# A convolution stack on one NeuronCore: other queues and another order for its DMA loads

## The chip, the cores and the metric

The kernel runs on one core of one Trainium2 chip. The metric is the time of one execution on the device in microseconds (us), taken as the median of several runs. A profile of one further execution tells where that time goes. PE is TensorE, DVE is VectorE, ACT is ScalarE, POOL is GpSimd and SP is SyncE. DMAs are issued by SP, ACT or POOL, each of which keeps its own queue of instructions in program order.

## The reference

Four layers follow one another on an image batch x of shape (4, 32, 32, 16) in float32. Each layer adds something to x that it computes from a group-normalised copy of x. Layers 0 to 2 are the same computation with other weights:

```python
first = jnp.einsum('ijpq,bpqc->bijc', M2, inputs)
K = jnp.transpose(G, (2, 3, 4, 0, 1, 5)).reshape(kh, kw, c, h * w * f)
shifted = lax.conv_general_dilated(inputs, K, window_strides=(1, 1), padding='SAME', ...)
shifted = shifted.reshape(b, h, w, h, w, f)
diff = jax.nn.relu(inputs[:, :, :, None, None, :] - shifted)
second = jnp.einsum('ijpq,bpqijc->bijc', W2, diff)
return first - L * second
```

M and Wp are 1024 x 1024 matrices and G holds 1024 different 3 x 3 x 16 x 16 filters, so every layer convolves the whole image with 16384 output channels. Layer 3 is a convolution with a 32 x 32 part of an impulse response, which comes from a quotient of two small 2-D polynomials by Fourier transforms, plus a constant tap h0:

```python
H_truncated = jnp.fft.rfft2(b, s=(l1, l2)) / jnp.fft.rfft2(a, s=(l1, l2))
...
Y = jnp.einsum('...hwi,ijhw->...hwj', X, H_full)
```

## The kernel before, in words

**A layer 0 to 2.** The 16384 channels are cut into 128 blocks of 128. For one block and one of the four images ("a pair" below) ten matmuls (line 336) accumulate in PSUM: the filters ga, gb and gn against the image tiles ims, which hold shifted copies of the image, so that the nine taps and 16 channels lie along the partitions. One DVE instruction (line 344) then takes the minimum with zero, multiplies by W and sums along the row. PSUM holds four such results, so PE can run four pairs ahead of DVE.

**Jobs.** conv_layer (line 301) goes through the blocks in jobs of eight, which is one chunk of G (GC = 8). The first two jobs take chunk 0 for images 0 and 1, then for images 2 and 3; the last two do the same with the last chunk; the fourteen jobs between take all four images, 32 pairs each. Inside a job the Python loop over k (0 to 7, one block each) also emits the loads, and since the schedule is written out by hand (manual_schedule), the order of emission is the order on every engine's queue:

- load_w (line 278) loads W for two blocks, 1 MB broadcast over eight groups of partitions, into one of six buffers. In the middle jobs it comes at even k, in the first two jobs at k = 4 and 6.
- load_g (line 239) loads a chunk of G: two halves each of ga and gb, 256 KB each, and g9, 512 KB broadcast. There are two buffers of ga and gb and one of g9. It comes at k = 1 of every job but the first, for the next job's chunk.
- prepare_g (line 257) comes at k = 6: POOL subtracts the middle tap from ga (line 266), ACT casts g9 into gn (line 270) and DVE forms its low part (line 273). PE needs all of them at the next job's start.
- first_term (line 180) is the layer's first einsum, beside the pairs: it loads M, multiplies on PE (line 199), stores the result ft to DRAM as fd in 16 DMAs (line 223), loads it back in another order as xf (line 226) and POOL adds x (line 231). It is a generator; a step of it is emitted after each block of the middle jobs.
- A second generator follows it: impulse_response in layer 0, toeplitz in layer 2.

**The images.** make_image (line 135) normalises two of the four images, writes them to DRAM (line 150 on SP, the edges in lines 154 and 155 on ACT) and loads the shifted copies back with 24 DMAs (line 166), half on SP and half on ACT. At the start of the program G chunk 0 and the first W are issued on SP ahead of all this; three more W follow the first image tiles (lines 506 to 517).

**The last layer's filter.** impulse_response (line 365) transforms on PE, divides on POOL and DVE, stores td to DRAM (line 441, ACT), loads it back transposed as v in 12 DMAs (lines 460 to 462, ACT), multiplies once more (line 470) and stores hd (lines 483 and 489, ACT), rows of 40 elements: 2048 runs of 160 bytes in each of four DMAs. After the v loads it yields three times, so that three blocks of pairs stand between them and line 470 in PE's order. load_toeplitz (line 495) loads hd into a tile t by eight DMAs of 256 runs of 640 bytes, alternately on SP and ACT. Three tiles are loaded by the toeplitz generator during layer 2, the other five in the tail, where 256 matmuls (line 564) finish the output.

**Semaphores of the DMAs.** SP's and ACT's DMAs share eight semaphores in rotation. A DMA waits until the one that used its semaphore before has landed. DMAs of POOL have eight semaphores of their own.

Of the kernel before, what the change touches and what calls it, by code (L numbers as in the profile page):

```python
# [37 lines left out]
P = 128  # L38
# [5 lines left out]
GC = 8  # L44
# [9 lines left out]
def conv_stack_kernel(ctx, tc, x, M, W, G, den, num, h0, cst, dft, one, idp, idq, out):  # L54
# [125 lines left out]
    def first_term(layer, xt):  # L180

        mts = [load_m(layer, 0)]
        yield
        py = small_psum()
        for b in range(B):
            nc.tensor.transpose(py[:, bass.ts(b, P)], yc[b // 2][:, b % 2, :], ident)
        yt = work.tile([P, 8, B, C], F32, tag="yt", name="yt")
        nc.vector.tensor_copy(yt, py.rearrange("k (b p c) -> k p b c", b=B, p=8))
        for pm in range(1, 4):
            mts.append(load_m(layer, pm))  # L190
            yield
        for _ in range(GC - 4):
            yield
        ft = work.tile([P, 2, 8, S], F32, tag="ft", name="ft")
        for part in range(2):
            pf = small_psum()
            for k in range(4):
                for h in range(2):
                    nc.tensor.matmul(  # L199
                        pf[64 * h : 64 * h + 64],  # L200
                        lhsT=yt[:, 4 * part + k].rearrange("k b c -> k (b c)"),
                        rhs=mts[k][:, h, :],
                        start=(k == 0),
                        stop=(k == 3),
                    )
            pv = pf.rearrange("k (cc p q) -> k cc p q", cc=2, p=8)
            if part == 0:
                nc.scalar.copy(ft, pv)
                mts = []
                for pm in range(4, 8):  # L210
                    yield
                    mts.append(load_m(layer, pm))
                for _ in range(GC - 4):
                    yield
            else:
                nc.vector.tensor_tensor(ft, ft, pv, ALU.add)

        fv = fd.rearrange("(p c) b h cc q -> h cc b c p q", p=8)
        for h in range(2):
            for b in range(B):  # L220
                for cc in range(2):
                    at = 64 * h + C * b
                    nc.scalar.dma_start(out=fv[h, cc, b], in_=ft[at : at + C, cc])  # L223
            yield
        xf = work.tile([P, B, NBLK], F32, tag="xf", name="xf")
        nc.scalar.dma_start(
            out=xf.rearrange("p b n -> p (b n)"), in_=fd.rearrange("p b h cc q -> p (b h cc q)")
        )
        yield
        xr = work.tile([P, B, NBLK], F32, tag="xr", name="xr")  # L230
        nc.gpsimd.tensor_tensor(xr, xt, xf, ALU.add)  # L231
        return xr
# [3 lines left out]
    def chunk(layer, ch):  # L236
        return layer + ch // (NBLK // GC), ch % (NBLK // GC)

    def load_g(layer, ch):
        layer, ch = at = chunk(layer, ch)  # L240
        if layer == 3 or at in gr:
            return
        ga = gs.tile([P, GC, P], F32, tag="ga", name="ga")
        gb = gs.tile([P, GC, P], F32, tag="gb", name="gb")
        g9 = gp.tile([P, GC, P], F32, tag="g9", name="g9")
        src = G[layer][:, bass.ts(ch, GC * P)]
        for half in range(2):
            rows = slice(64 * half, 64 * half + 64)
            nc.sync.dma_start(out=ga[rows].rearrange("r n m -> r (n m)"), in_=src[:64])
            nc.sync.dma_start(out=gb[rows].rearrange("r n m -> r (n m)"), in_=src[64:P])  # L250
        nc.sync.dma_start(
            out=g9.rearrange("r n m -> r (n m)"),
            in_=src[P : P + C].unsqueeze(0).to_broadcast([8, C, GC * P]),
        )
        gr[at] = ga, gb, g9
# [19 lines left out]

    wts = []

    def load_w():

        layer, at = divmod(len(wts), NBLK // 2)  # L280
        if layer == 3:
            return
        cc, q = divmod(2 * at, S)
        wt = wp.tile([P, 2, S * S], F32, tag="w", name="w")
        src = W[layer][cc, :, q : q + 2, :].rearrange("p k m -> p (k m)")
        nc.sync.dma_start(
            out=wt.rearrange("p k m -> p (k m)"),
            in_=src.unsqueeze(1).to_broadcast([8, C, 2 * S * S]),
        )
        wts.append(wt)  # L290

    todo = []

# [7 lines left out]
    def conv_layer(layer, xt, finish, side=()):  # L301
# [14 lines left out]
        for job, (blks, batches) in enumerate(jobs):  # L316
            pairs = job < 2, job >= len(jobs) - 2
            for k, blk in enumerate(blks):
                if any(pairs):

                    if k in ((4, 6) if job != len(jobs) - 2 else (0, 2)):
                        load_w()
                elif k % 2 == 0:
                    load_w()
                if job:
                    if k == 1:
                        load_g(layer, blk // GC + 1)
                    if k == 6:
                        prepare_g(layer, blk // GC + 1)
                wt = wts[64 * layer + blk // 2][:, blk % 2, :]  # L330
                for b in batches:
                    pt = pair_psum()
                    for n, (w, im) in enumerate(zip(gt[layer, blk // GC], ims[b // 2])):
                        for half in range(2):
                            rows = slice(64 * half, 64 * half + 64)
                            nc.tensor.matmul(  # L336
                                pt[:, half, :],
                                lhsT=w[rows, blk % GC, :],
                                rhs=im[rows, :, b % 2, :, :S],
                                start=n == 0,  # L340
                                stop=n == 2,
                            )
                    junk = junkp.tile([P, S * S], F32, tag="junk", name="junk")
                    nc.vector.scalar_tensor_tensor(  # L344
                        junk,
                        pt.rearrange("p h m -> p (h m)"),
                        0.0,
                        wt,
                        ALU.min,
                        ALU.mult,  # L350
                        accum_out=acc[b // 2][:, b % 2, blk : blk + 1],
                    )
                    step()
                if not any(pairs):
                    next(beside, None)
            if pairs[1]:
                a = batches[0] // 2
                two = slice(2 * a, 2 * a + 2)
                nc.vector.tensor_tensor(xn[:, two], result["xr"][:, two], acc[a], ALU.add)
                drain()  # L360
                todo.append(finish(a, xn))
                step()
        return xn

    def impulse_response():
# [81 lines left out]
        with tc.tile_pool(name="fs2", bufs=1) as fs:  # L447
# [9 lines left out]
            rows = td.rearrange("k r p (u m) -> u (k r) p m", u=4)  # L457
            for u in range(4):
                g = 32 * u
                nc.scalar.dma_start(out=v[g : g + 1], in_=rows[u, 0:1])  # L460
                nc.scalar.dma_start(out=v[g + 1 : g + 2], in_=rows[u, 32:33])
                nc.scalar.dma_start(out=v[g + 2 : g + 32], in_=rows[u, 2:32])
            yield
            yield
            yield
            for part in range(4):
                pq = pair_psum()
                for h in range(2):
# [11 lines left out]
                )  # L480
                yield
            nc.gpsimd.tensor_tensor(hs[:, :, :, 0], hs[:, :, :, 0], h0s, ALU.add)
            nc.scalar.dma_start(
                out=hd[:, :8].rearrange("(n m) r -> n m r", m=4), in_=hs[:, 0, :4, S:]
            )
            for h in range(2):
                for l in range(2):
                    n = 64 * (2 * h + l)
                    nc.scalar.dma_start(
                        out=hd[n : n + 64, 8:].rearrange("m (q r) -> q m r", r=PITCH),  # L490
                        in_=hs[32 * l : 32 * l + 32, h],
                    )
            yield

    def load_toeplitz(k):

        t = tp.tile([P, C, TQ * PITCH], F32, tag="t", name="t")
        hv = hd.rearrange("(j i) t -> i j t", j=C)
        for p in range(8):
            at = 8 + k * TQ * PITCH - p  # L500
            (nc.sync, nc.scalar)[p % 2].dma_start(
                out=t[p * C : (p + 1) * C], in_=hv[:, :, at : at + TQ * PITCH]
            )
        return t

    load_g(0, 0)
    load_w()
    images = [make_image(a, xs) for a in range(2)]
    for _ in range(4):
        next(images[0])  # L510
    prepare_g(0, 0)
    todo.append(images[0])
    drain()
    for _ in range(3):
        load_w()
    todo.append(images[1])
    step()
    xs = conv_layer(0, xs, make_image, impulse_response())
# [17 lines left out]

    def toeplitz():
        for k in range(3):
            ts.append(load_toeplitz(k))
            yield  # L540

    xs = conv_layer(2, xs, norm3, toeplitz())
# [113 lines left out]
```

## Time and profile before

| what | value |
|---|---|
| median of 3 runs | 3216.66 us (3215.99 to 3217.17) |
| the profiled execution: its time | 3216.64 us |
| the profiled execution: its span | 3214.8 us |
| PE busy | 3148.2 us (98%), 15852 matmuls |
| DVE busy | 2054.8 us (64%) |
| ACT busy | 75.7 us (2%) |
| POOL busy | 171.9 us (5%) |
| mean granted clock of TensorE | 0.994 |
| moved by DMA | 322.18 MB, 100 GB/s in the mean |
| SP's queue | 302.69 MB, 39.2% of 16 engines' span |
| ACT's queue | 17.04 MB, 3.4% |

The profile is one execution. Its busy times are unions of the instructions' spans on an engine; an engine that waits for a semaphore or issues a DMA is not counted as busy, and a q behind the engine's name (SPq, ACTq) marks such sequencer time. The chain goes back from the last instruction to whatever released it, step by step. In the groups and waits, "A <- B" says that A stood until B was done. "PEclk" and the clock column are the share of full speed that the throttle granted TensorE.

### The profile page before, as it was taken

The page shows a single profiled execution, that of the slowest core. Times are in us where ns is not written, and L with a number is a line of the kernel's source. Part 1 is how long each engine was busy: PE and PEld are TensorE (multiplying, and loading weights), DVE is VectorE, ACT ScalarE, POOL GpSimd, SP SyncE. Part 2 cuts the span into 40 slices and gives each one's busy share as a digit, 9 for nine tenths or more (in the row PEclk, how much of TensorE's full clock was granted, in tenths as well). Part 3 has the DMA queues.
Part 4 walks back from the last instruction along what each step waited for, and adds up shares of the span by engine and source line. Part 5 has one row for each costly group of instructions (what it writes and reads, how often), then busy time and mean ns, then how long its engine had stood idle before and what let it go on. Part 6 is the DMA issues. An engine that isn't in the chain of part 4 may idle for free.

```text
span 3214.8 us, 38408 instructions
## 1 busy us (share of the span) xinstructions
PE 3148.2 (98%) x15852; PEld 1678.7 (52%) x15852; DVE 2054.8 (64%) x3294; ACT 75.7 (2%) x98; POOL 171.9 (5%) x124
## 2 busy tenths in 40 slices
PE   6999999999999999999999999999989999999998
PEld 3545566666666544444544445454444444444445
DVE  4666765666666766666666666766656666666660
ACT  0000000000000000000000000000000000000000
POOL 0002310000000000000000000000000000000000
PEclk9999999999999999999999999999999999999999
DMA  6544344343333554333433343365473343333306
GB/s 148 156 115 116 88 109 94 86 103 88 88 98 90 107 154 118 99 89 88 99 96 86 86 105 87 80 143 144 99 127 89 98 99 89 87 99 92 86 1 85
DMA packets 106383, 322.18 MB, mean 100 GB/s; under 512 B 29214, under 2 KB 59360, under 8 KB 81632
## 3 DMA queue, kind: packets, MB, share of 16 engines
q1 hardware_dynamic: 68608, 302.69, 39.2%
q10 hardware_dynamic: 37600, 17.04, 3.4%
q8 instruction: 124, 2.03, 0.3%
q14 instruction: 51, 0.42, 0.1%
HBM read 313.01 MB, written 6.68 MB: 99 GB/s over the span
## 4 chain that ended last, share of the span: by engine, by line
PE 94%; DMA 4%; DVE 1%; ACTq 0%; issue 0%; SPq 0%; POOL 0%; ACT 0%; DVEq 0%; POOLq 0%
PE pt L336 90%; PE pt L564 2%; DMA t<-hd 1%; DMA img<-y 1%; DMA im<-img 1%; PE pt L199 1%; DMA td<-s 1%; DMA v<-td 0%; DMA fd<-ft 0%; DVE junk L344 0%; DMA h0s<-in_h_dram 0%; PE pt L470 0%; ACTq L223 0%; PE pt L387 0%; POOL hs L452 0%
## 5 line engine op out<-in xcount | busy, mean ns | idle before, releaser
L344 DVE SCALAR_TENSOR_TENSOR junk<-pt,w 128x1024 f32<-128x1024 f32 x1536 | 1880.8, 1224 | 1031.7 <-PE pt L336 1017.4
L336 PE MATMUL pt<-im,ga 64*128 64x512 f32 x6144 | 1834.4, 592 | 38.0 <-DMA im<-img 20.5
L336 PE MATMUL pt<-im,gb 64*128 64x512 f32 x6144 | 1824.4, 589 | 0.9 <-DMA im<-img 0.9
L336 PE MATMUL pt<-im,gn 64*128 64x512 f32 x3072 | 1487.7, 807 | 1.9 <-DMA im<-img 1.9
L336 PEld LDWEIGHTS pt<-im,gb 64*128 64x128 f32 x6144 | 706.5, 186 | 737.7 <-issue 705.0
L336 PEld LDWEIGHTS pt<-im,ga 64*128 64x128 f32 x6144 | 708.6, 188 | 422.8 <-DVE junk L344 246.6
L336 PEld LDWEIGHTS pt<-im,gn 64*128 64x128 f32 x3072 | 355.3, 186 | 295.4 <-issue 290.2
L266 POOL TENSOR_TENSOR ga<-ga,cs 128x1024 f32<-128x1024 f32 x48 | 113.4, 2362 | 2215.5 <-DMA ga<-in_G_dram 2153.5
L273 DVE TENSOR_TENSOR gn<-g,gn 32x1024 fp32r<-32x1024 f32 x96 | 118.0, 1229 | 34.3 <-ACT gn L270 32.3
L344 DVE DVE_READ_ACCUMULATOR junk<-pt,w 128x1 f32 x1536 | 127.3, 83 | 0.0
L270 ACT CAST gn<-g 128x1024 fp32r<-128x1024 f32 x48 | 50.2, 1047 | 2318.7 <-DMA g<-in_G_dram 2020.4
L564 PE MATMUL pt<-t,y 128*128 128x512 f32 (+3 forms) x256 | 70.4, 438 | 0.0
L564 PEld LDWEIGHTS pt<-t,y 128*128 128x128 f32 x256 | 44.2, 193 | 26.2 <-issue 16.2
L571 DVE TENSOR_TENSOR xo<-xo,pt 128x512 f32<-128x512 f32 x1 | 0.7, 689 | 70.8 <-PE pt L564 70.8
L199 PE MATMUL pt<-mt,yt 128*64 128x512 f32 x96 | 21.9, 598 | 0.0
L231 POOL TENSOR_TENSOR xr<-x,xf 128x512 f32<-128x512 f32 x3 | 3.8, 1271 | 294.5 <-DMA xf<-fd 294.5
L470 PE MATMUL pt<-v,inv 64*128 64x512 f32 x16 | 8.6, 656 | 7.5 <-DMA v<-td 7.5
L199 PEld LDWEIGHTS pt<-mt,yt 128*64 128x64 f32 x96 | 6.4, 136 | 13.7 <-issue 9.4
L147 POOL COPY e<-y 32x612 f32<-32x612 f32 x6 | 4.2, 693 | 171.7 <-DVE y L146 171.7
L104 PE MATMUL pt<-s,cs 128*128 128x2 f32 x16 | 3.3, 276 | 9.7 <-DVE s L101 9.7
L408 POOL TENSOR_TENSOR H<-H,d 128x256 f32<-128x256 f32 (+1 forms) x10 | 8.2, 825 | 66.6 <-DVE d L413 66.3
L408 POOL TENSOR_TENSOR t<-s 128x256 f32<-128x256 f32 (+1 forms) x15 | 11.3, 754 | 0.0
(57 smaller groups left out, 141.0 us busy)
## 6 DMA issues: line engine op xcount, KB each, us to landing
w<-in_W_dram SPq DMA_DIRECT2D x192, 1024.0 KB
ga<-in_G_dram SPq DMA_DIRECT2D x96, 256.0 KB
gb<-in_G_dram SPq DMA_DIRECT2D x96, 256.0 KB
g<-in_G_dram SPq DMA_DIRECT2D x48, 512.0 KB
mt<-in_M_dram SPq DMA_DIRECT2D x24, 512.0 KB
t<-hd SPq DMA_DIRECT2D x32, 160.0 KB
t<-hd ACTq DMA_DIRECT2D x32, 160.0 KB
im<-img ACTq DMA_DIRECT2D x72, 67.5 KB
```

The lines of the kernel that those rows point to most:

```text
L104: nc.tensor.matmul(pm[:, :2], lhsT=avg, rhs=s, start=True, stop=True)
L147: nc.gpsimd.tensor_copy(ye[a][96:, :, :, 1:, :], ys[a][96:, :, :, :3, :])
L199: nc.tensor.matmul(pf[64 * h : 64 * h + 64], lhsT=yt[:, 4 * part + k].rearrange("k b c -> k (b c)"), rhs=mts[k][:, h, :], start=(k == 0), ...
L231: nc.gpsimd.tensor_tensor(xr, xt, xf, ALU.add)
L266: nc.gpsimd.tensor_tensor(gv, gv, mid.unsqueeze(1).to_broadcast([P, GC * 8, C]), ALU.subtract)
L270: nc.scalar.copy(gn, g9)
L273: nc.vector.tensor_tensor(lo, g9[r : r + 32], lo.bitcast(F32), ALU.subtract)
L336: nc.tensor.matmul(pt[:, half, :], lhsT=w[rows, blk % GC, :], rhs=im[rows, :, b % 2, :, :S], start=n == 0, stop=n == 2,)
L344: nc.vector.scalar_tensor_tensor(junk, pt.rearrange("p h m -> p (h m)"), 0.0, wt, ALU.min, ALU.mult, accum_out=acc[b // 2][:, b % 2, blk : ...
L408: mul = lambda o, u, w: nc.gpsimd.tensor_tensor(o, u, w, ALU.mult)
L470: nc.tensor.matmul(pq[:, h, :], lhsT=inv[two], rhs=v[two, bass.ts(part, 8)].rearrange("g p m -> g (p m)"), start=True, stop=True,)
L564: nc.tensor.matmul(pov[:, :, 8 * cc :], lhsT=y3[:, cc, 31 - dq : 31 - dq + S, :].rearrange("p q b -> p (q b)"), rhs=t[:, :, q * PITCH : q ...
```

## The change

It has four parts, and the arithmetic stays as it is.

1. At the start, the gb halves of G chunk 0 are issued by ACT instead of SP. The first W is no longer issued ahead of the image's store: it is cut into two halves, the first behind that store and ahead of the im loads, the second behind them.
2. In a layer's first job, load_g for chunk 1 is called at k = 3, ahead of the W of k = 4 and 6; until now it came in the second job at k = 1, behind them.
3. The stores fd, the loads xf and v and the stores hd go from ACT's queue to POOL's. Between the v loads and line 470 there are six yields instead of three.
4. The first three Toeplitz tiles, which were issued by SP and ACT in turn, are issued by POOL alone. Those of the tail stay as they were.

POOL's queue thus gets, in each of layers 0 to 2, 16 fd stores and the xf load ahead of line 231's add; in layer 0 also 12 v loads and 5 hd stores; in layer 2 also 24 Toeplitz loads, between that add and the next chunk's line 266. The diff:

```diff
@@ first_term
-                    nc.scalar.dma_start(out=fv[h, cc, b], in_=ft[at : at + C, cc])
+                    nc.gpsimd.dma_start(out=fv[h, cc, b], in_=ft[at : at + C, cc])
             yield
         xf = work.tile([P, B, NBLK], F32, tag="xf", name="xf")
-        nc.scalar.dma_start(
+        nc.gpsimd.dma_start(
             out=xf.rearrange("p b n -> p (b n)"), in_=fd.rearrange("p b h cc q -> p (b h cc q)")
         )
@@ load_g
-    def load_g(layer, ch):
+    def load_g(layer, ch, other=None):
...
-            nc.sync.dma_start(out=gb[rows].rearrange("r n m -> r (n m)"), in_=src[64:P])
+            (other or nc.sync).dma_start(out=gb[rows].rearrange("r n m -> r (n m)"), in_=src[64:P])
@@ load_w
-    def load_w():
+    def load_w(parts=1):
...
-        nc.sync.dma_start(
-            out=wt.rearrange("p k m -> p (k m)"),
-            in_=src.unsqueeze(1).to_broadcast([8, C, 2 * S * S]),
-        )
         wts.append(wt)
+        n = 2 * S * S // parts
+        for k in range(parts):
+            nc.sync.dma_start(
+                out=wt.rearrange("p k m -> p (k m)")[:, bass.ts(k, n)],
+                in_=src[:, bass.ts(k, n)].unsqueeze(1).to_broadcast([8, C, n]),
+            )
+            yield
@@ conv_layer
-                        load_w()
+                        list(load_w())
                 elif k % 2 == 0:
-                    load_w()
-                if job:
-                    if k == 1:
-                        load_g(layer, blk // GC + 1)
-                    if k == 6:
-                        prepare_g(layer, blk // GC + 1)
+                    list(load_w())
+                if k == (3 if job == 0 else 1):
+                    load_g(layer, blk // GC + 1)
+                if job and k == 6:
+                    prepare_g(layer, blk // GC + 1)
@@ impulse_response
-                nc.scalar.dma_start(out=v[g : g + 1], in_=rows[u, 0:1])
-                nc.scalar.dma_start(out=v[g + 1 : g + 2], in_=rows[u, 32:33])
-                nc.scalar.dma_start(out=v[g + 2 : g + 32], in_=rows[u, 2:32])
-            yield
-            yield
-            yield
+                nc.gpsimd.dma_start(out=v[g : g + 1], in_=rows[u, 0:1])
+                nc.gpsimd.dma_start(out=v[g + 1 : g + 2], in_=rows[u, 32:33])
+                nc.gpsimd.dma_start(out=v[g + 2 : g + 32], in_=rows[u, 2:32])
+            for _ in range(6):
+                yield
...
-            nc.scalar.dma_start(
+            nc.gpsimd.dma_start(
                 out=hd[:, :8].rearrange("(n m) r -> n m r", m=4), in_=hs[:, 0, :4, S:]
             )
...
-                    nc.scalar.dma_start(
+                    nc.gpsimd.dma_start(
                         out=hd[n : n + 64, 8:].rearrange("m (q r) -> q m r", r=PITCH),
@@ load_toeplitz
-    def load_toeplitz(k):
+    def load_toeplitz(k, queues=(nc.sync, nc.scalar)):
...
-            (nc.sync, nc.scalar)[p % 2].dma_start(
+            queues[p % len(queues)].dma_start(
                 out=t[p * C : (p + 1) * C], in_=hv[:, :, at : at + TQ * PITCH]
             )
@@ the start of the program
-    load_g(0, 0)
-    load_w()
+    load_g(0, 0, nc.scalar)
+    w0 = load_w(2)
     images = [make_image(a, xs) for a in range(2)]
     for _ in range(4):
         next(images[0])
+    next(w0)
     prepare_g(0, 0)
     todo.append(images[0])
     drain()
+    next(w0)
     for _ in range(3):
-        load_w()
+        list(load_w())
@@ toeplitz
-            ts.append(load_toeplitz(k))
+            ts.append(load_toeplitz(k, (nc.gpsimd,)))
```

## Prediction

> **What bounds the kernel now.** I read the page's chain first, then busy time by stretch, then chain, waits and timeline around each stretch in which PE is not full.
>
> ```profile
> PE 94%; DMA 4%; DVE 1%; ACTq 0%; issue 0%; SPq 0%; POOL 0%; ACT 0%; DVEq 0%; POOLq 0%
> ```
>
> The end is set by PE. A (block, image) pair is ten matmuls; the chain gives 3720 in 732.38 us, so 1.97 us a pair and 62.8 us a job of 32 pairs. The change touches none of these 15360 matmuls (3024 us). It can only touch what PE loses:
>
> ```profile
> 0.00:34.90 34.90, 5.76 (x12) 2.52 (x13) 6.83 (x17) 3.64 (x5) 6.16 (x10) 1.00 0.68 154
> 71.30:125.00 53.70, 49.31 (x235) 35.00 (x236) 30.96 (x49) 1.04 (x1) 2.35 (x1) 0.94 0.68 153
> 440.00:520.00 80.00, 72.52 (x352) 48.04 (x350) 42.00 (x68) 5.68 (x7) 7.34 (x4) 0.94 0.43 96
> 2296.00:2368.00 72.00, 58.95 (x300) 28.12 (x296) 35.21 (x56) 1.04 (x1) 3.60 (x2) 0.93 0.83 113
> ```
>
> The columns are stretch, length, then PE, PEld, DVE, ACT, POOL busy, granted clock, DMA share, GB/s. These four hold nearly all of PE's idle time; in 520 to 1052 and 1166 to 2068 PE is busy throughout. The chain names what is late in the first three:
>
> ```profile
> 10.96 12.46 DMA img<-y
> 46.44 14.34 DMA img<-y
> 101.56 4.39 issue
> 474.46 13.55 DMA v<-td
> ```
>
> The image's store needs 12.46 us because G and the first W stand ahead of it. The landings in the trace (a DMA's last semaphore update) show it: g9 at 13.32, W at 22.57, the store at 23.41. The gap at 101.56 is G chunk 1: issued at 71.0 behind two W, landed at 101.03. At 480.7 PE stands 7.48 us in line 470 until v lands. The fourth, by waits:
>
> ```profile
> ACT gn L270 <- DMA t<-hd: 120.6, 1, 120.6
> DVE gn L273 <- ACT gn L270: 15.9, 1, 15.9
> PE pt L336 <- DVE junk L344: 13.0, 1, 13.0
> ```
>
> ```profile
> 2341.79 21.18 ACTq L501 DMA_DIRECT2D t<-hd  x12
> 2363.06 1.04 ACT L270 CAST gn<-g 128x1024 fp32r<-128x1024 f32 x1 [120.56 <-DMA t<-hd]
> ```
>
> ACT can't cast gn until it has issued its Toeplitz loads, which wait for free semaphores; DVE stands in line 273, and PE runs out of PSUM. Each long pause also costs clock: the records show half speed from 105.0 to 111.8, 483.9 to 494.1 and 2357.8 to 2371.4.
>
> **What the Trainium skill says.** (1) "DMA: Bandwidth & Descriptors", section "Issuing engines are not separate DMA queues": all queues share the same 16 engines, another queue saves only issue time. The trace agrees: the v load that ACT issued at 474.46 landed at 488.02, with SP's W (486.89). (2) "Perfetto Trace Analysis", section "DMA Instruction — SWDGE (GPSIMD)": a GpSimd DMA occupies its cores until the last descriptor is written, so the next POOL instruction waits. No run here shows one. (3) "TensorE: Matmul & The Clock Gate", section "What's actually happening": half clock after an idle window of about 3.4 us. The trace agrees: half clock begins 3.4 us after the gap at 101.56.
>
> **The head.** In the new order x, ga, ga, g9 stand in SP's queue and gb, gb in ACT's: the same 1.5 MB on the same engines, so g9 still lands near 13.3. The store (issued 10.96, unchanged) then lands 0.84 after it (23.41 less 22.57), and with the edges I take 15.5. Half of W follows: two W landed 8.19 apart (43.56, 51.75), so a half is 4.1 and ends near 18.4, ahead of the im loads in the ring. These took 8.7 from first landing (25.98) to last (34.72): 18.9 + 8.7 = 27.6. First gn matmul at 27.8 instead of 34.91: 7.1 gained (8.1 if the half W is harmless, 5 if it holds back the edges).
>
> The second image gains less. Behind its store's turn stand a half and three W (28.7 us) instead of three: 27.6 + 28.7 = 56.3, +1.1 for the store, +10.7 for its im loads (60.78 to 71.49) = 68. PE ends job 0 near 62.5 and idles in pieces until 68; job 1 starts 3.5 earlier than before. Then chunk 1, now ahead of W and landed near 76, no longer stops it: 4.39 plus 2.9 (105.95 to 111.81 at half speed) disappear. Against that I set 1.5 for the clock in the new pause (0 to 3). DVE's first product of job 2 moves from 110.20 to 69 + 31.4 + 1.5 = 101.9: **8.3 gained** (5 to 11). The fifth and sixth W, now behind G, land near 85 and 93, before job 2 wants them. In layers 1 and 2 the first two jobs (32.8 and 31.4 us) have no such stall, so G there is worth nothing; W moved back by 8.3 keeps some 18 us of cover in layer 1 (the first landed at 1123, wanted near 1149).
>
> **The price of a GpSimd DMA** is not in the trace. Bounds from ACT's issues: fd 0.44, t 0.46, v (960 runs) 0.88 us below; above, an hd store of 2048 runs held ACT 11.04 us, 5.4 ns a run. I take 0.3 us plus 4 ns a run, an estimate inside these: fd (128 runs) 0.8, t (256) 1.3, v 4.1 and 0.4, hd 8.5. Below nothing is excluded: the ring doesn't shorten a transfer.
>
> **v and hd.** Three more yields put line 470 3 x 7.85 = 23.6 us later in PE's order, from 480.1 to 503.7, less 8.3 = 495. POOL's memset ends at 462.1 less 8 = 454; the 12 loads take 4 x 4.1 + 8 x 0.4 = 20, with waits for the eight GpSimd semaphores and two W in flight they land by 480 to 495. So 7.48 idle and 3.0 of half clock (488.15 to 494.10) disappear, less 1.5 of remaining wait: **9.0 gained** (2 to 10.5). The ga subtraction behind them (2.36 us) is done by 483, wanted at 495. Behind hd it is closer: hd starts at 523 after the fourth part (495 + 3 x 7.85 + 4.5), 1.3 + 4 x 8.5 = 35 us, then ga until 561; PE wants it at job 9, 495 + 62.8 + 4.5 for line 470's own matmuls = 562. **0**, with 1 us of margin; that cover is gone from 4.2 ns a run on.
>
> **fd, xf and Toeplitz.** Leaving ACT frees the gn cast: 81.66 less 62.83 less 3.58 (line 199) = 15.25 us of loss in that job. But now POOL does 16 fd, xf, xr, 24 t and only then ga, which PE wants at 2362.3 (positions of the kernel before). xr depends on fd landing between W; layer 0's undisturbed case took 36.8 from the job's G issue (238.3) to xr (275.1), so here 2332, and 1.3 for the add plus slow fd: t starts at 2335.5. Issuing takes 24 x 1.3 = 32; the last issue waits for the 16th landing, and t landed 1.5 us apart when alone: 24, plus W in between, which took 8.2 each. I put the last issue at 2372 (bounds 2361, t first; 2392, t starved while W runs, as ACT's last four were: issued from 2359, landed 2381 to 2393). ga ends 2375: a stall of 12.7 and 2.5 of clock, 15.2. What goes on ACT comes back on POOL: **0** (+12 to -21). In layers 0 and 1 fd costs nothing: ga follows 24 us before it is wanted (276.4, 305.7).
>
> **Sum.** 3216.64 (the profiled execution; its span is 3214.8, the median of the runs 3216.66) - 8.3 - 9.0 + 0 + 0 = 3199.3, say **3200**.
>
> **Rivals.** (a) All stalls vanish, GpSimd cheap and t ahead of W: 3216.6 - 10 - 10.5 - 12 = 3184. For it: ACT's issues of 0.44 us. Against: the fd, xf and t chain that POOL inherits.
> (b) t starved by W, line 270's wait replaced by one of ga on POOL of 33 + 3 us: 3200 + 21 = 3221. For it: the four loads above.
> (c) Slower: descriptor writing holds POOL. From 4.2 ns a run ga of job 9 is late, from about 6 ns the sum turns: hd 4 x 12.6 + 1.8 = 52 (16 late + 2.5), t 24 x 1.84 = 44 (20 late + 2.5, 7 more than before): 3200 + 18.5 + 7 = 3225; at 8 ns, 3200 + 35 + 19 = 3254. For it: hd's 8192 short runs; against: v's 960 runs in 0.88 us on ACT.
>
> **Chances.** Forecast (3193 to 3208) 0.35; (a) 0.18; (b) 0.14; (c) 0.33. About 0.2% (6.4 us) is what a measurement of this kernel can tell from no change: faster 0.53, same 0.14, slower 0.33. The range, 3184 to 3245, cuts (c) at some 7 ns.
>
> **What would show it.** Head: img store landed by 16, first gn matmul near 28, job 1 near 68, no gap at its end. Line 470: no wait over 3 us. POOL: 24 t issues over some 35 us and ga after them; a PE wait for ga near 2345 (2362 less 17), in place of that for gn. Wrong if hd stores hold POOL over 8.7 us each, or if t takes under 1 us each and lands despite W.

## The result and the profile after

The changed kernel takes 3218.62 us in the median of five runs (3213.68 to 3221.65), the kernel before 3216.66 (five runs, 3214.52 to 3219.25). The ratio is 1.0001, 95% interval 0.9988 to 1.0015: no change that can be measured, where 3200 was forecast. The profiled execution took 3213.88 us with a span of 3212.1 (before: 3216.64 and 3214.8), so it shows 2.8 us less than before, at the fast end of the runs.

The page's chain, then the stretches in the same columns as in the prediction (stretch, length, PE, PEld, DVE, ACT, POOL busy, granted clock, DMA share, GB/s):

```profile
PE 95%; DMA 4%; DVE 1%; POOL 0%; issue 0%; ACT 0%; SPq 0%; POOLq 0%; DVEq 0%
```

```profile
0.00:28.60 28.60, 5.74 (x12) 2.46 (x13) 6.83 (x17) 3.64 (x5) 6.16 (x10) 1.00 0.69 164
28.60:69.30 40.70, 36.69 (x165) 17.84 (x165) 23.01 (x45) 1.31 (x3) 0.69 (x1) 0.99 0.62 146
69.30:105.00 35.70, 35.70 (x168) 27.44 (x170) 22.95 (x35) 1.04 (x1) 2.35 (x1) 0.92 0.65 150
440.00:520.00 80.00, 80.00 (x411) 57.31 (x409) 50.52 (x80) 4.43 (x5) 15.33 (x17) 1.00 0.50 109
2280.00:2377.00 97.00, 68.87 (x340) 32.96 (x338) 42.97 (x68) 1.04 (x1) 28.29 (x44) 0.86 0.67 117
```

On POOL, unlike on SP and ACT, a DMA's row counts as busy, so the 28.29 us of POOL in the last line include its DMAs.

Three of the four stalls went as forecast. PE starts at 28.6 instead of 34.9. The gap ahead of the third job is gone (35.70 busy in 35.70 us), and so is the one at line 471 (before: line 470; 80.00 in 80.00 us). The fourth has grown. Between 2280 and 2377 PE is idle for 28.13 us, where it lost 13.05 before, and another engine is named. The waits from 2330 to 2380 (us in total, times, longest):

```profile
POOL t L502 <- DMA t<-hd: 41.8, 15, 11.5
...
PE pt L338 <- POOL ga L266: 28.1, 1, 28.1
```

The chain of that stretch (start, length, what) gives the order, from the add of line 231 to PE's restart:

```profile
2313.55 1.27 POOL xr L231
2314.82 3.29 POOL t L502 x6
2318.11 24.44 DMA t<-hd
2342.55 0.28 issue
2342.84 24.96 DMA t<-hd
...
2370.09 2.36 POOL ga L266
```

The Toeplitz loads stand between xr and ga in POOL's program. POOL issues eight at once and then one for each that lands. The chain runs through two landings of 24.44 and 24.96 us, and ga comes last. PE stood from 2344.36 to 2372.49.

The distance between the first DVE product of one job and that of the next books the whole difference:

| stretch | before | after | difference |
|---|---|---|---|
| start of layer 0's fourth job (head, images, G chunk 1) | 174.69 | 167.83 | -6.9 |
| its eighth and ninth jobs together (v, line 470, hd) | 141.40 | 129.93 | -11.5 |
| layer 2's fifth job (fd, xf, Toeplitz, ga) | 81.66 | 96.60 | +14.9 |
| start of the last product | 3133.22 | 3129.81 | -3.4 |

Layers are numbered 0 to 2, as ahead of the prediction, and a layer's jobs are counted from the first; where an expectation below says "layer 3", it means layer 2, and its "jobs 7 and 8" are the eighth and ninth. All other jobs have the lengths they had.

### The profile page after: what moved, and what is told of

The parts are those of the page before. It is cut to its first block, busy times and chain, and to the rows that moved or that the text cites. A ratio compares the mean times of both kernels' runs of the same rounds, so it can differ in the third digit from the quotient of the medians.

```text
span 3212.1 us, 38474 instructions
## 1 busy us (share of the span) xinstructions
PE 3145.4 (98%) x15852; PEld 1725.2 (54%) x15852; DVE 2054.9 (64%) x3294; ACT 75.7 (2%) x98; POOL 224.4 (7%) x216
## 4 chain that ended last, share of the span: by engine, by line
PE 95%; DMA 4%; DVE 1%; POOL 0%; issue 0%; ACT 0%; SPq 0%; POOLq 0%; DVEq 0%
PE pt L338 91%; PE pt L567 2%; DMA t<-hd 2%; PE pt L199 1%; DMA img<-y 1%; DMA im<-img 1%; DMA fd<-ft 0%; DVE junk L346 0%; DMA img<-e 0%; PE pt L389 0%; PE pt L432 0%; POOL t L502 0%; POOL fd L223 0%; PE pt L471 0%; DMA x<-in_x_dram 0%
## 5 line engine op out<-in xcount | busy, mean ns | idle before, releaser
L338 PE MATMUL pt<-im,ga 64*128 64x512 f32 x6144 | 1693.5, 592 | 44.9 <-POOL ga L266 28.1
L338 PE MATMUL pt<-im,gb 64*128 64x512 f32 x6144 | 1684.7, 589 | 2.4 <-DMA im<-img 2.4
L338 PE MATMUL pt<-im,gn 64*128 64x512 f32 x3072 | 1357.4, 806 | 1.4 <-DMA im<-img 1.4
L338 PEld LDWEIGHTS pt<-im,gb 64*128 64x128 f32 x6144 | 689.1, 186 | 665.0 <-issue 636.2
L338 PEld LDWEIGHTS pt<-im,ga 64*128 64x128 f32 x6144 | 691.5, 188 | 417.8 <-DVE junk L346 224.8
L223 POOL DMA_DIRECT2D fd<-ft x48 | 25.2, 532 | 219.7 <-DVE ft L216 211.0
L502 POOL DMA_DIRECT2D t<-hd x24 | 13.5, 564 | 41.8 <-DMA t<-hd 41.8
L410 POOL TENSOR_TENSOR H<-H,d 128x256 f32<-128x256 f32 (+1 forms) x10 | 8.3, 825 | 66.6 <-DVE d L415 66.2
```

What stands on the lines that cost most here:

```text
L223: nc.gpsimd.dma_start(out=fv[h, cc, b], in_=ft[at : at + C, cc])
L338: nc.tensor.matmul(pt[:, half, :], lhsT=w[rows, blk % GC, :], rhs=im[rows, :, b % 2, :, :S], start=n == 0, stop=n == 2,)
L410: mul = lambda o, u, w: nc.gpsimd.tensor_tensor(o, u, w, ALU.mult)
L502: queues[p % len(queues)].dma_start(out=t[p * C : (p + 1) * C], in_=hv[:, :, at : at + TQ * PITCH])
```

## The experiments

After the result, my theory A was that ga is late only because it stands behind 24 issues on POOL, and that eight semaphores make the last issue wait for the 16th landing, which comes slowly while W and G use the same DMA engines. Theory B: transfers from GpSimd's queue are slow in themselves. Theory C: fd and xf on POOL make the whole chain late, Toeplitz loads or not. Rival (c) of the prediction, that writing descriptors holds POOL, fell with the profile after: an hd store holds POOL for 1.05 us, not 8.5 (last section).

**Part 1 and 2 alone (e1_head).** The kernel after with parts 3 and 4 undone: fd, xf, v and hd on ACT, three yields, Toeplitz on SP and ACT.

```diff
-                    nc.gpsimd.dma_start(out=fv[h, cc, b], in_=ft[at : at + C, cc])
+                    nc.scalar.dma_start(out=fv[h, cc, b], in_=ft[at : at + C, cc])
...
-            ts.append(load_toeplitz(k, (nc.gpsimd,)))
+            ts.append(load_toeplitz(k))
```

> Parts 1 and 2 of the change alone; fd, xf, v, hd and all Toeplitz loads stay on ACT and SP as before. Theory A (the parts add up, and the loss comes from POOL's order in layer 2 alone): DVE's first product of layer 0's third job near 104.2 us as in the changed kernel, 6 to 7 us of gain kept to the end, the job after line 199's second round in layer 2 still 81.7 us long; in all 3216.7 - 6.5 = 3210. Rival (the head's gain is given back later, because G and W come in another order in all layers): 3214 or more.

Measured: 3209.24 us against 3215.26, ratio 0.9979 (0.9972 to 0.9985). Parts 1 and 2 are worth 6 us by themselves.

**v and hd alone (e2_v_hd).** The kernel before with these DMAs on GpSimd and six yields.

```diff
-                nc.scalar.dma_start(out=v[g : g + 1], in_=rows[u, 0:1])
+                nc.gpsimd.dma_start(out=v[g : g + 1], in_=rows[u, 0:1])
...
-            yield
-            yield
-            yield
+            for _ in range(6):
+                yield
```

> The v loads and hd stores alone on POOL, with six yields; all else as before. Theory A: no pause of PE in line 470, layer 0's jobs 7 and 8 together 11.5 us shorter than before, and nothing else moves: 3216.7 - 11.5 = 3205. Rival (writing descriptors of short runs holds POOL, so that ga of the next job comes late): a wait of PE for ga of several us in layer 0's job 8 and a gain under 6 us, 3211 or more.

Measured: 3205.97 us, ratio 0.9969 (0.9958 to 0.9981), 9.3 us. The fifth job of layer 2 keeps its loss there (81.30 us), as in e1 (79.86).

**fd and xf alone (e10_fd_xf).** The kernel before with line 223 and line 226 on GpSimd.

```diff
-                    nc.scalar.dma_start(out=fv[h, cc, b], in_=ft[at : at + C, cc])
+                    nc.gpsimd.dma_start(out=fv[h, cc, b], in_=ft[at : at + C, cc])
...
-        nc.scalar.dma_start(
+        nc.gpsimd.dma_start(
             out=xf.rearrange("p b n -> p (b n)"), in_=fd.rearrange("p b h cc q -> p (b h cc q)")
```

> The kernel before with fd and xf on GpSimd's queue and nothing else. If it is the pile of waiting issues ahead of ScalarE's gn cast (16 fd, xf and 12 Toeplitz loads in one order, each fd and each load waiting for a landing) that costs 15 us in the fifth job of layer 3, taking fd and xf out of it lets the Toeplitz loads start 20 us earlier, the cast runs before TensorE wants it, and the job takes 66 to 69 us instead of 81.7: 3200 to 3204. If GpSimd's queue is slow enough to hold xf, xr and with them ga, part of the stall comes back at line 266: 3206 to 3216.

Measured: 3201.34 us against 3215.09, ratio 0.9957 (0.9945 to 0.9969); the job takes 66.61 us. ACT's timeline in that kernel (start, us, instruction, idle before it):

```profile
2240.86 0.31 ACTq L501 DMA_DIRECT2D t<-hd  x1
...
2241.21 98.93 ACTq L501 DMA_DIRECT2D t<-hd  x11
2340.26 1.05 ACT L270 CAST gn<-g 128x1024 fp32r<-128x1024 f32 x1 [98.26 <-DMA t<-hd]
```

The cast still stands behind all twelve Toeplitz loads of ACT, but these no longer stand behind fd, which waits for DVE's ft until 2308. ACT runs ahead: its first Toeplitz load goes out at 2240.86, not at 2341.79. The twelve now take 99 us instead of 21, as they wait for the semaphores that they share with SP, and the cast still runs at 2340 instead of 2363, some 6 us before DVE comes to line 273 (2347.80). Taking fd and xf off ACT was enough to free the cast. The queue of GpSimd didn't make xr late: it ran at 2340.64 against 2344.51 before. Theory C falls.

**The Toeplitz loads back (e3_t_back).** The kernel after without part 4.

```diff
-            ts.append(load_toeplitz(k, (nc.gpsimd,)))
+            ts.append(load_toeplitz(k))
```

> The changed kernel with the first three Toeplitz tiles issued by SP and ACT again; fd, xf, v, hd stay on POOL. Theory A (ga stands on POOL behind 24 Toeplitz issues): no wait for ga; gn's cast is behind twelve Toeplitz issues on ACT again, but these no longer stand behind fd and xf and start some 30 us earlier, so PE loses 0 to 10 us in that job instead of 30: 3188 to 3198. Rival C (fd and xf on POOL make that chain late): the loss of some 30 us stays, 3215 or more.

Measured: 3185.6 us (3183.89 to 3187.5), ratio 0.9908 (0.9893 to 0.9923); the job takes 66.61 us instead of 96.60. So part 4 costs 30 us and undoes all that the rest gains. The rest of the change, measured in three pieces (e1, e2, e10), gives 0.21, 0.31 and 0.43%, in sum 0.95%, against 0.92% here: the pieces add up.

**One load a step (e4_t_spread).** The kernel after with one Toeplitz DMA after each block, still on GpSimd, so that ga finds only three ahead of it in the stretch.

```diff
         for k in range(3):
-            ts.append(load_toeplitz(k, (nc.gpsimd,)))
-            yield
+            t = tp.tile([P, C, TQ * PITCH], F32, tag="t", name="t")
+            ts.append(t)
+            for p in range(8):
+                at = 8 + k * TQ * PITCH - p
+                nc.gpsimd.dma_start(
+                    out=t[p * C : (p + 1) * C], in_=hv[:, :, at : at + TQ * PITCH]
+                )
+                yield
```

> The changed kernel with the 24 Toeplitz loads on POOL as there, but one a block instead of eight a block, so that none waits for a semaphore and ga stands behind at most a few. Theory A: no wait of PE for ga, the job in layer 2 is 66.4 to 68 us long instead of 96.6; 30 us less than the changed kernel, span 3182, time 3184 to 3189. Rival B (a transfer of GpSimd's queue is slow in itself, over 3 us each, and holds the rest up wherever it stands): the 24 transfers slow W or ga in three jobs, and less than 15 us is won, 3200 or more.

Measured: 3187.59 us, ratio 0.9911 (0.9895 to 0.9928); the job takes 66.61 us. POOL's timeline:

```profile
2318.48 1.69 POOL L547 DMA_DIRECT2D t<-hd  x3
2320.18 2.37 POOL L266 TENSOR_TENSOR ga<-ga,cs 128x1024 f32<-128x1024 f32 x1
```

**ga ahead of the loads (e6_ga_first).** Four empty steps ahead of the Toeplitz generator; the loads go out in bunches of eight as in the kernel after.

```diff
     def toeplitz():
+        for _ in range(4):
+            yield
         for k in range(3):
```

> The changed kernel, but the Toeplitz loads come four steps later, so that ga stands ahead of all 24 of them in GpSimd's order; all still go out in bunches of 8 on GpSimd's queue. Theory A (the stall is ga's place behind the issues, nothing else): ga runs at about 2316 right behind xr, TensorE doesn't stop, the job takes 66.6 us instead of 96.6 and the kernel 3184 to 3190, though the loads themselves land as slowly as before. Theory C (fd and xf on GpSimd's queue make the chain late, so ga would be late without the Toeplitz loads too): part of the stall, 5 us or more, stays. Theory B (the queue's transfers load the engines so that W or G come late): the stall becomes one of W or G, over 5 us.

Measured: 3186.67 us, ratio 0.9902 (0.9887 to 0.9917); the job takes 66.61 us. POOL's timeline:

```profile
2316.32 1.27 POOL L231 TENSOR_TENSOR xr<-x,xf 128x512 f32<-128x512 f32 x1 [2.44 <-DMA xf<-fd]
2317.55 2.36 POOL L266 TENSOR_TENSOR ga<-ga,cs 128x1024 f32<-128x1024 f32 x1
2319.85 4.48 POOL L502 DMA_DIRECT2D t<-hd  x8
2335.35 0.57 POOL L502 DMA_DIRECT2D t<-hd  x1 [11.02 <-DMA t<-hd]
```

Here the loads are as slow as ever: the first is issued at 2319.85 and the last at 2372.54. Nobody is behind them that PE wants soon, and the stall is gone. fd and xf are where they were in the kernel after, which refutes theory C a second time. The place of ga decides, and the slow loads only set how long it is kept.

**Two W less (e5_two_w_less).** This kernel leaves out two of the four W tiles of that job.

```diff
+                elif layer == 2 and job == 4 and k in (4, 6):
+                    wts.append(wts[-1])
                 elif k % 2 == 0:
```

> The changed kernel, but two of the four W tiles of the fifth job of layer 3 are not loaded: its blocks 4 to 7 are multiplied with the W tile of blocks 2 and 3, so that part of the computation is changed. Theory A (the Toeplitz loads land slowly because W's transfers hold the same engines, and ga waits behind the issues): with two of W's 8-us transfers gone from the stretch the 24 loads land some 1.5 to 2 us apart, the last of them is issued by about 2350 instead of 2369.5 and TensorE idles 0 to 8 us instead of 28. Theory B (GpSimd's queue is slow in itself): the loads stay 3 us apart, the stall stays at 20 to 28 us. By A the execution takes 3185 to 3195, by B 3210 to 3216.

Measured: one execution, 3184.4 us; no stall in the job (66.61 us). The waits:

```profile
POOL t L504 <- DMA t<-hd: 12.3, 15, 1.8
```

The 15 waits of POOL for a landing shrink from 41.8 to 12.3 us. From the first landing to the last, the loads land 1.3 us apart instead of 2.5 (trace, issue and last landing):

```
          kernel after            two W less
t  #1   2314.77 -> 2330.41     2315.53 -> 2319.39
t #16              2369.23                2340.49
t #24   2369.51 -> 2387.84     2340.78 -> 2350.02
```

Same queue, same descriptors, nearly twice the pace: theory B falls, A stands. This is what the Trainium skill says in "DMA: Bandwidth & Descriptors", section "Issuing engines are not separate DMA queues": DMAs end up on the same 16 engines and interleave, whoever issues them. The trace agrees: taking away 2 MB of SyncE's loads brought the last of GpSimd's issues forward by 28.7 us. Two W alone would take 16.4 us (8.2 each); the rest is in good part the next W and G's chunk, which in the kernel after are issued from 2343.35, into the Toeplitz loads, and here after them. The stretch from the first to the last issue shows it (columns as above; kernel after, then two W less):

```profile
2314.70:2369.50 54.80, 29.66 (x152) 14.51 (x148) 22.16 (x34) 0.00 (x0) 12.98 (x24) 0.81 0.81 122
2315.50:2341.30 25.80, 25.80 (x135) 12.80 (x134) 18.74 (x29) 0.00 (x0) 13.52 (x25) 1.00 1.01 121
```

With two W less the Toeplitz loads have the engines to themselves and fill them (1.01). In the kernel after, SyncE's W and G put 3.36 MB into the same stretch and their packets took 40.3% of the 16 engines' time, 22 us of the 29 by which the stretch is longer. The engines also stood idle for 0.19 of it, some 10 us; why is not shown. (The Toeplitz packets themselves took some 4 us less than with two W less.)

**The bunch of loads on the old queues (e8_before_spread).** The kernel before with one Toeplitz load a step on SP and ACT in turn, fd and xf still on ACT.

```diff
-            ts.append(load_toeplitz(k))
-            yield
+            for p in range(8):
+                (nc.sync, nc.scalar)[p % 2].dma_start(
+                    out=t[p * C : (p + 1) * C], in_=hv[:, :, at : at + TQ * PITCH]
+                )
+                yield
```

> The kernel before, its 24 Toeplitz loads still on SyncE's and ScalarE's queues, but one a step instead of eight. In the kernel before the gn cast on ScalarE stood behind these loads and fd (15.25 us lost in that job). With fd and xf on GpSimd and the Toeplitz loads back on their queues that loss was gone (66.61 us). If what costs is the bunch of Toeplitz loads ahead of the cast in ScalarE's order, spreading them does the same without GpSimd: the job takes 66 to 70 us and the kernel 3201 to 3206. If it is the fd loads, whose issues wait on ScalarE for landings behind W (2308 to 2341 in the kernel before), 5 us or more of the stall stay: 3206 to 3217.

Measured: 3202.47 us against 3217.72, ratio 0.9948 (0.9931 to 0.9965); the job takes 66.61 us. ACT's timeline has one Toeplitz load ahead of the cast, which runs at 2325, not 2363:

```profile
2324.65 0.46 ACTq L544 DMA_DIRECT2D t<-hd  x1
2325.20 1.05 ACT L270 CAST gn<-g 128x1024 fp32r<-128x1024 f32 x1 [82.32 <-issue]
```

So fd and xf alone on ACT don't hurt either. Either half of the pile may leave: without fd (e10) or without the bunch (e8) the cast is in time, and GpSimd isn't needed for that.

**The head again (e7_w_behind, e9_one_behind).** Both start from e3_t_back, where the second image's store is issued at 40.5 and lands at 59.2, behind three W. e7 leaves one W ahead of the store, puts one behind it and one behind that image's im loads; e9 moves only the last, right behind the store.

```diff
@@ make_image, behind the edges (e9)
+        if a == 1 and len(wts) == 3:
+            list(load_w())
@@ the start of the program (e9)
-    for _ in range(3):
+    for _ in range(2):
         list(load_w())
```

> The kernel with the Toeplitz prefetch back on SyncE's and ScalarE's queues (run third), and of the three whole W tiles that it asks for ahead of the second image's store one stays ahead, one goes behind the store and one behind that image's im loads. If W's backlog is what holds the second image (its store was issued at 40.5 and landed at 59.2, behind W), TensorE's idle 4 us at 61.7 to 69 and the half-clock stretch after it go, and the second job starts 3 to 5 us earlier. Against it: the W tile of blocks 6 and 7 then lands at about 64 instead of 58.2, and VectorE, which wants it at about 54, becomes the bound of that job. I expect 3181 to 3185 against 3185.6, with VectorE's wait for W grown from 4 to about 8 us; if W's own 8 us a tile is the whole bound of the head, no change.

> The kernel with the Toeplitz prefetch back on SyncE's and ScalarE's queues (run third, 3185.6), with only the last of its three W tiles moved: right behind the second image's store and ahead of that image's im loads. Moving two of them starved VectorE of W (it waited 22.8 us for W in the head against 4.3). If W and the image just share a fixed amount of transfer, what the image gains the tile of blocks 6 and 7 loses: store landed at about 51 instead of 59, im loads done at about 65 instead of 70, that W tile at about 62 instead of 58, and the time within 2 us of 3185.6. If there is slack in the image's backlog, 3181 to 3184. If VectorE is already the bound of the first job, 3187 to 3190.

Measured: e7 3193.78 us (0.9925, 0.9911 to 0.994), 8 us above e3's median. Each was measured beside its own runs of the kernel before, and the intervals of the two ratios overlap, but the runs of e7 and e3 don't, and in the profiles the third job begins at 113.8 instead of 104.5. DVE runs dry of W, and PE of PSUM:

```profile
DVE junk L351 <- DMA w<-in_W_dram: 22.8, 2, 16.9
...
PE pt L343 <- DVE junk L351: 14.6, 2, 14.0
```

I had named that risk and put it at 8 us of waiting; it was 22.8, because the last W landed at 76.1, not 64. e9: 3184.19 us (3182.14 to 3185.68), ratio 0.9916 (0.9899 to 0.9932). Its store landed at 50.36, the im loads at 67.9 and that W at 59.6. The ranges of e9 and e3 overlap, so no gain over e3 is shown. The best versions, e3, e4, e6 and e9 (0.9902 to 0.9916), can't be told apart; all beat both kernels by some 0.9%.

## Why the prediction was wrong

**Head: right, a little high.** Forecast -8.3, measured -6.9 in the profile and 6 us in e1. One pair of profiles is not enough here: layer 0's fourth job begins at 174.7 to 177.1 in the four traces with the old head (before, e2, e8, e10) and at 167.8 to 171.6 in six with the new one (after, e1, e3 to e6), 6.6 us apart in the mean. The store landed at 14.41 (forecast 15.5), but half the W held back the edges, as in the case that the text allowed: they landed at 18.45 and 19.25. PE's first gn matmul came at 28.62 (27.8). Where the rest went: I set 1.5 us for the clock in the new pause before the second job; the records show half speed from 68.33 to 75.16, some 3 us. This pause also varies. Of its wait for im, PE shows 4.0 us in the profile after, 4.1 in e3 and 6.5 in e4, and the third job begins at 104.2, 104.5 and 108.0. The prediction's "nearly all of PE's idle time" was 54 of 66.6 us; most of the rest lies at the ends of the layers and in the tail, which the change leaves alone.

**Gap at the end of job 1: right.** It is gone; chunk 1 landed at 78.6 (forecast 76).

**v, line 470: right.** Forecast -9.0, measured -11.5 in the profile; e2 gained 9.3, with the same 11.5 in the two jobs of its profile. v had landed by 479.7, and PE shows no wait there; the 1.5 us of remaining wait that I set didn't come.

**hd: 0 was right, its working wrong.** I priced a GpSimd DMA at 0.3 us plus 4 ns a run and left 1 us of margin. The four stores took 4.20 us together instead of 34, and ga followed at 529.36, some 30 us before the tenth job began (564.8). The 0 doesn't vouch for the price: it held because a store costs far less than that price, not because the margin of 1 us was right. Rival (c), a third of my chance, rested on this price.

**fd, xf and Toeplitz: the step that failed.** The text says "What goes on ACT comes back on POOL: **0** (+12 to -21)"; it measured -15. Three of its four links held. The cast on ACT was freed, worth 15.25 by the text and 13.8 us in e10. POOL inherited the order xr, 24 t, ga, and PE waited for ga at line 266. The loads began at 2314.8; the forecast's 2335.5 in the positions of before is 2317 here, 18.35 earlier. What failed is the length of the issue: "24, plus W in between", 36.5 us in all; it was 54.7. The 24 us for 16 landings is right when nothing interferes (25 us in e5), but the term for what interferes had room for about one and a half W. The trace shows W in flight from 2314.25 to 2333.10, 2329.95 to 2358.14 and 2346.89 to 2387.61, and G from 2343.35 to 2377.13. The stall was 28.1 us plus about 2 of clock, 30.0 in the job's length (96.60 against 66.61), where I had 15.2. This term alone makes a forecast of 3200 into 3215; rival (b), which was just this ("t starved by W", 3221, a stall of 36), came true in its mechanism and had 0.14. I chose the middle of a range whose pessimistic end had a row of its own in the profile: ACT's last four loads, issued from 2359 and landed 22 to 30 us later under W.

**The rivals.** (a), 3184 with all stalls gone, is what e3, e4 and e6 measure, to within 4 us; only the place of the loads denied it. (c) fell with the price. The price mattered little even for the fourth stall: the 24 issues themselves took 13.5 of the 54.7 us, and the rest was the wait that eight semaphores make, which tie the 24th issue to the 16th landing.

What stays open: the five runs of the kernel after spread over 8 us, and only the one near their fast end was traced. The head alone varies by some 4 us over the six traces named above; whether the length of the fourth stall makes the rest wasn't tried.

## What to carry to other kernels

When a DMA is moved to another engine's queue, ask which computing instruction stands behind it in that engine's order and when it is wanted. With eight semaphores the hold here was not the time to issue but the wait for the landing eight places ahead of the last issue, and that depended on what else used the DMA engines (e5). Ask also what the engine that it leaves will now do sooner: without fd, ACT issued its first Toeplitz load 101 us earlier (e10). A prefetch that nobody needs soon belongs behind the work that is needed, or in single steps between it (e4, e6: 30 us for a few lines moved). A change of several parts is measured part by part: here three gave 0.9% together and one took all of it back.

## What the runs showed of the hardware

**A GpSimd DMA costs its engine little.** One Toeplitz and one fd row of the page's groups (x count, then busy us, mean ns), and POOL's timeline at the four hd stores:

```profile
L223 POOL DMA_DIRECT2D fd<-ft x48 | 25.2, 532 | 219.7 <-DVE ft L216 211.0
L502 POOL DMA_DIRECT2D t<-hd x24 | 13.5, 564 | 41.8 <-DMA t<-hd 41.8
```

```profile
525.14 4.20 POOL L490 DMA_DIRECT2D hd<-hs  x4 [25.48 <-issue]
529.36 2.37 POOL L266 TENSOR_TENSOR ga<-ga,cs 128x1024 f32<-128x1024 f32 x1
```

fd (128 runs) 0.53 us, t (256) 0.56, v (960) 0.86, hd (2048) 1.05: about 0.5 us plus 0.3 ns a run. The same hd stores had held ACT for 28.15 us in e1. The next instruction on POOL starts as the row ends (529.34 and 529.36). The Trainium skill has it in "Perfetto Trace Analysis", section "DMA Instruction — SWDGE (GPSIMD)", that such a row ends with the last descriptor and not with the data. The trace agrees: rows of 0.56 us, landings 15 to 28 us after the issue.

**Short idle pieces cost clock too.** The section "What's actually happening" of "TensorE: Matmul & The Clock Gate" gives half clock after an idle window of about 3.4 us. In the head of the kernel after no single gap before the second job is longer than 1.74 us (0.89, 1.74 and 1.36 in 7 us; half speed begins within the third), and the records still show half speed for 6.83 us. e9, with 1.89 and 1.29 us, shows 3.41 us of it. Here the measurement decides: half clock came without a single gap of 3.4 us. What share of idle time is enough is not worked out from these traces.
